# Second layer of a convolution and state-space network: token 6's input by compact sums, three products in column tiles, and a new written order

## The chip, the cores and the metric

The kernel runs on one core of a Trainium2 chip. The metric is the device time of one execution in microseconds (us), and the median of several runs stands for it. The engines are TensorE (PE), VectorE (DVE), ScalarE (ACT), GpSimd (POOL) and SyncE (SP), which here only issues transfers (DMAs). Each engine works through its own queue in order, and semaphores make it wait for the others. Matrix products land in PSUM, eight banks of 128 x 512 float32.

## The reference: what is computed

Two layers run on x of shape 8 x 128 x 128 x 128. The change touches only the second, which is this (cut):

```python
y = conv3x3(x, conv_w) + conv_b
seq = y.reshape(B * H * W, 8, 16)            # 8 tokens of 16 values
# in_proj, causal conv1d over tokens, silu -> xc [n, 8, 32]; z from the other half
dt, Bm, Cm = split(xc @ x_proj_w.T)          # 1, 16, 16 per token
dt = softplus(dt * dt_proj_w + dt_proj_b)
dA = exp(dt[..., None] * A)                  # [n, 8, 32, 16]
dBx = dt[..., None] * Bm[:, :, None, :] * xc[..., None]
h = dA[t] * h + dBx[t];  ys[t] = (h * Cm[t][:, None, :]).sum(-1)   # t = 0..7
out = ((ys + D * xc) * silu(z)) @ out_proj_w.T
out = x + silu(groupnorm(out))               # 4 groups, over the whole image
```

A sequence is one line of an image along its width: 128 values are 8 tokens of 16. For each of the 131072 sequences there is a state of 32 channels x 16, stepped through eight tokens from zero.

## The kernel before

The first layer ends at about 1950 us. The second works in 256 blocks, each of 4 image rows in all 128 channels (512 sequences). A block's state for one token is 32 x 16 = 512 rows of 512 sequences. It is cut into two chunks of 128 partitions x 2 x 512 (a chunk is called s, s = 2 t + half, so s runs from 0 to 15). The functions are steps, and the tuple ORDER gives the order in which one turn of the loop calls them: an entry is a step, the block it works on relative to the turn's block i, and its arguments. All five engines follow this order in their own queues (the schedule is manual), so a step's place is decided by hand, and nothing reorders it.

For a block, in the order of the data:

- conv (L137, in the helper _conv_taps): 9 taps, each a full-array product of 128 x 128 weights with 512 columns, into the only bank of "pm". biased and turn copy and transpose it.
- project_x, project_z, project_dt (L749, L761, L771) and project_bc (L789) give xc, z, dt and the rows of B and C. silu (ACT), softplus (L776), inputs u = dt * xc (L781, POOL), states (L796) take them out of PSUM.
- lay_states (L804) spreads each token's 16 rows of B ("bb") or C ("cc") over 128 partitions by transfers of 256 KB. store_inputs and lay_inputs (L814, L821) do so with u for the chunks that POOL injects.
- spread_a and spread_u (both L830): two products with 32 rows of the array each put dt * A, or u, of one chunk into one of three PSUM slots (2 banks each). Even chunks use the array's rows 0 to 63, odd ones rows 64 to 127.
- exps (L841, ACT) makes dA in place. inject makes h = u * B on DVE from PSUM (L853), or on POOL from a laid out copy (L851) for the chunks in BY_POOL = (4, 5, 10). decay multiplies dA by the earlier token's h in place (L861), add sums it into h (L866). weigh (L872, POOL) multiplies h by C.
- collect (L936): for each token, column-tiled products (32 columns of the array each, four side by side) sum over the 16 states into "yps".
- Tokens 0 and 7 are short cuts. Token 0's whole term and token 7's input term need no state: (sum over n of C B) * u. lay_ends and lay_own (L882, L891) gather the rows of B, C and u compactly, end_products (L896, POOL) multiplies B and C, ends_sum (L905, PE) sums over n, own_terms (L911, DVE) multiplies by u, own_add (L918, PE) adds into yps. Token 7's decayed part is dA7 * (C7 h6): weigh first, then decay (L859).
- skip (L929) starts yps with D * xc, gated (L943, DVE) multiplies by silu(z), project_out (L951) and result give the output. After an image's last block norm_of forms the group norm; last_load to last_store finish an earlier image beside the work. The last image is finished at the end.

PSUM holds the three slots (6 banks), pm (1) and yps (1). h tiles have 9 buffers, hc tiles 8, used in turn.

Of the kernel before, what the change touches and what calls it, by code (L numbers as in the profile page):

```python
# [16 lines left out]
P = 128  # L17
C = 128
# [21 lines left out]
def _fields(widths):  # L40
# [13 lines left out]
    ("half", NH * L), ("group", P), ("ends", 4 * NH * DI), ("place", 2 * NH * P),  # L54
# [13 lines left out]
def _constants():  # L68
# [4 lines left out]
    def put(c, fields, name, v):  # L73
# [34 lines left out]
    quarter, end = i % 4, i // (P // 2)  # L108
    put(c1, C1, "ends", np.stack([
        ((quarter == q) & (end == e))[:, None] & np.ones(DI, bool)[None, :] for q in range(4) for e in range(NH)], 1))  # L110
    put(c1, C1, "place", np.stack([
        (i // DI == h)[:, None] & (k[:, None] == i[None, :] // LP) & (i % LP == (0, LP - 1)[h % NH])[None, :]
        for h in range(2 * NH)], 1))
    put(c1, C1, "half", np.stack(
        [(i % LP)[:, None] + hf * LP == np.arange(L)[None, :] for hf in range(NH)], 1))
# [482 lines left out]
def layer1(ctx, tc, x1, w1, c1, out):  # L598
# [33 lines left out]
    ends = cf("ends").rearrange("p (q e d) -> p q e d", e=NH, d=DI)  # L632
# [56 lines left out]
    hcp = ctx.enter_context(tc.tile_pool(name="l1_hc", bufs=8))  # L689
# [6 lines left out]
    st8 = [{} for _ in blocks]  # L696
    xins, stats, gns, tails = {}, {}, {}, []
    LAST = (3, 6)
    BY_POOL = (4, 5, 10)
# [22 lines left out]
    def conv(i, k):  # L722
        d = st8[i]
        if k == 0:
            d["pm"] = misc()
        xin, lo = d["xin"]
        _conv_taps(nc, [d["pm"]], convw, [xin], lo, blocks[i][1], 1, k, k + 1)
# [17 lines left out]
    def project_x(i, slot):  # L745
        d = st8[i]
        d["ps"] = pair(slot)
        for hf in range(NH):
            nc.tensor.matmul(d["ps"][:, hf], m_xh[:, hf, :], d["yT"], start=True, stop=True)  # L749
# [18 lines left out]
    def project_dt(i, hf):  # L768
        d = st8[i]
        d["pm"] = misc()  # L770
        nc.tensor.matmul(flat(d["pm"]), m_dtf, d["xc"][:, hf, :], start=True, stop=True)  # L771
# [26 lines left out]
    def lay_states(i, hf, k):  # L798

        d, name = st8[i], ("bb", "cc")[k]  # L800
        v = wk2.tile([P, LP, N], F32, name=name)
        for t in range(hf * LP, (hf + 1) * LP):
            if t != (L - 1, 0)[k]:
                nc.sync.dma_start(  # L804
                    v[:, t % LP, :],
                    d["bc"[k]][t * DS:(t + 1) * DS, :].unsqueeze(1).broadcast_to([DS, 8, N]))
        d[name, hf] = v
# [35 lines left out]
    def state_row(i, name, t):  # L843
        return st8[i][name, t // LP][:, t % LP:t % LP + 1, :].broadcast_to([P, GP, N])
# [10 lines left out]
    def decay(i, s):  # L855
        d = st8[i]
        da = d["da", s]
        if s >= GP * (L - 1):
            nc.vector.tensor_mul(d["hc", s], da, d["hc", s])  # L859
        else:  # L860
# [12 lines left out]

    def lay_ends(i):
# [3 lines left out]
        d["bcs"] = wk1.tile([P, 2, C], F32, name="bcs")  # L878
        for k in range(2):
            src = d["bc"[k]].rearrange("p (q c) -> p q c", c=C)  # L880
            for e, t in enumerate((0, L - 1)):
                nc.sync.dma_start(d["bcs"][e * P // 2:(e + 1) * P // 2, k, :], src[t * DS:(t + 1) * DS])  # L882

    def lay_own(i):
        d = st8[i]
        d["us"] = wk1.tile([P, N // 2], F32, name="us")
        for e, l in enumerate((0, LP - 1)):
            u = d["u", e].rearrange("(d l) n -> l d n", l=LP)
            for h in range(2):
                a = (h * NH + e) * DI  # L890
                nc.sync.dma_start(d["us"][a:a + DI, :], u[l][:, h * (N // 2):(h + 1) * (N // 2)])  # L891

    def end_products(i):
        d = st8[i]
        d["cb"] = wk1.tile([P, C], F32, name="cb")
        nc.gpsimd.tensor_mul(d["cb"], d["bcs"][:, 0, :], d["bcs"][:, 1, :])  # L896

    def ends_sum(i):

        d = st8[i]  # L900
        d["pm"] = misc()
        for q in range(4):
            for e in range(NH):
                a = (q // 2 * NH + e) * DI
                nc.tensor.matmul(  # L905
                    d["pm"][a:a + DI, q % 2, :], ends[:, q, e, :], d["cb"], start=True, stop=True)
# [287 lines left out]
```

## Time and profile before

| | us |
|---|---|
| median of 3 runs | 13790.77 (13786.41 to 13790.79) |
| the profiled execution's own time | 13787.05 |
| its span, first to last instruction | 13785.2 |
| mean granted PE clock | 0.991 of full |
| first state operation of the second layer (inject) | 1968.6 |
| last block's output | 13707.1 |
| DVE decay, add (L861, L866), mean of one | 1.224, 1.220 |
| DVE inject from PSUM (L853), mean of one | 1.219 |
| POOL weigh (L872), mean of one | 2.365 |
| ACT exp (L841), mean of one; table load | 1.008; 1.283 |

A line of the profile names the engine, the line of the kernel, the operation and the tiles as out<-in, then how many and how long. Lengths of neighbouring operations on one engine overlap a little (an operation's start may lie before the end of the one ahead), so that what one costs in a full queue is the distance from its start to the next start. PE's lengths overlap much more, and products on different parts of the array run at once. "32*128" is a product that uses 32 of the array's rows and all its columns, "128*32" one with 32 of its columns.

### The profile page before, as it was taken

To read this page: it belongs to the slowest core of one execution; us is meant where nothing else is said; L and a number is where in the kernel's file an instruction comes from. 1 tells how busy PE (TensorE), PEld (TensorE's weight loads), DVE (VectorE), ACT (ScalarE), POOL (GpSimd) and SP (SyncE) were. 2 spreads that over 40 slices of the span, in tenths; PEclk is the share of its full clock that TensorE was granted. 3 is DMA by queue.
4 is the path that set the end of the run, shared out by engine and by line. 5 is a ranking of instruction groups with operands and counts; after the bars stand their busy time and mean duration, and the time that the engine had idled before them with its cause. 6 is when DMAs were issued, how large, how long until landed. Compare 5 with 4: busy or idle time off the path is not lost. (4 is left out here: it accounts for less than half of the span.)

```text
span 13785.2 us, 222858 instructions
## 1 busy us (share of the span) xinstructions
PE 13399.1 (97%) x80938; PEld 5420.6 (39%) x80938; DVE 12207.0 (89%) x11963; ACT 8884.5 (64%) x10881; POOL 12418.5 (90%) x6788
## 2 busy tenths in 40 slices
PE   9999999999999999999999999999999999999997
PEld 5676663333333333333333333333333333333332
DVE  3343359999999999999999999999999999999997
ACT  3454366666666666666666666666666666666665
POOL 6766669999999999999999999999999999999997
PEclk9999999999999999999999999999999999999998
DMA  4544456666667666666766666666666676667666
GB/s 134 159 133 126 142 133 139 139 137 137 147 155 158 153 152 155 156 156 149 158 154 157 154 153 155 156 156 151 156 156 155 150 158 154 158 148 158 154 156 179
DMA packets 1224332, 2078.57 MB, mean 151 GB/s; under 512 B 149568, under 2 KB 378944, under 8 KB 1215040
## 3 DMA queue, kind: packets, MB, share of 16 engines
q1 hardware_dynamic: 1222656, 2061.57, 64.5%
q8 instruction: 640, 10.49, 0.3%
q14 instruction: 460, 3.77, 0.1%
q10 hardware_dynamic: 576, 2.74, 0.1%
HBM read 822.20 MB, written 234.88 MB: 77 GB/s over the span
## 5 line engine op out<-in xcount | busy, mean ns | idle before, releaser
L872 POOL TENSOR_TENSOR hc<-h,cc 128x1024 f32<-128x1024 f32 x3584 | 8377.6, 2365 | 523.5 <-PE pm L905 409.5
L841 ACT ACTIVATE s<-s 128x1024 f32<-128x1024 f32 x3584 | 3589.5, 1008 | 2879.1 <-PE s L830 2727.0
L830 PE MATMUL s<-dt,m_a 32*128 32x512 f32 x14336 | 3967.9, 638 | 25.8 <-DVE h L866 13.9
L866 DVE TENSOR_TENSOR h<-s,h 128x1024 f32<-128x1024 f32 x3072 | 3726.2, 1220 | 71.4 <-DVE s L861 1.4
L861 DVE TENSOR_TENSOR s<-s,h 128x1024 f32<-128x1024 f32 x3072 | 3738.0, 1224 | 2.8 <-ACT s L841 2.7
L853 DVE TENSOR_TENSOR h<-s,bb 128x1024 f32<-128x1024 f32 x2816 | 3431.9, 1219 | 224.6 <-PE s L830 111.8
L830 PE MATMUL s<-u,l_ct 32*128 32x512 f32 x11264 | 3164.1, 638 | 143.7 <-DVE h L853 134.6
L137 PE MATMUL pm<-xin,l_wt 128*128 128x508 f32 (+1 forms) x4608 | 2341.6, 617 | 6.1 <-DVE wk L652 5.4
L936 PE MATMUL yps<-hc,l_ct 128*32 128x512 f32 x14336 | 1852.6, 602 | 2.7 <-ACT away L969 2.7
L851 POOL TENSOR_TENSOR h<-ud,bb 128x1024 f32<-128x1024 f32 x768 | 1808.5, 2370 | 11.5 <-DMA ud<-uw 11.5
L830 PEld LDWEIGHTS s<-dt,m_a 32*128 32x128 f32 x14336 | 1105.0, 183 | 1432.6 <-DVE h L866 532.5
L830 PEld LDWEIGHTS s<-u,l_ct 32*128 32x128 f32 x11264 | 867.8, 184 | 1371.9 <-DVE h L853 555.3
L137 PEld LDWEIGHTS pm<-xin,l_wt 128*128 128x128 f32 x4608 | 771.5, 189 | 1478.2 <-issue 1260.5
L841 ACT ACT_TABLE_LOAD x774 | 993.0, 1283 | 29.1 <-DVE h L853 11.0
L936 PEld LDWEIGHTS yps<-hc,l_ct 128*32 128x32 f32 x14336 | 362.3, 109 | 1140.6 <-issue 1061.6
L781 POOL TENSOR_TENSOR u<-dt,xc 128x512 f32<-128x512 f32 x512 | 649.9, 1269 | 77.5 <-ACT dt L776 46.8
L776 ACT ACT_TABLE_LOAD x511 | 655.6, 1283 | 50.5 <-PE pm L771 9.8
L859 DVE TENSOR_TENSOR hc<-s,hc 128x1024 f32<-128x1024 f32 x512 | 622.1, 1215 | 2.8 <-ACT s L841 2.8
L771 PE MATMUL pm<-xc,m_dt 128*128 128x512 f32 x1024 | 583.8, 652 | 1.4 <-ACT yT L743 0.7
L951 PEld LDWEIGHTS pm<-m_o,ym 128*128 128x128 f32 x4096 | 476.5, 191 | 194.5 <-ACT dt L776 192.7
L918 PE MATMUL yps<-own,l_ct 128*32 128x256 f32 x8192 | 542.2, 382 | 0.1
L789 PE MATMUL pm<-xc,m_bc 128*32 128x512 f32 x4096 | 539.3, 598 | 2.3 <-ACT all_b L796 1.4
(195 smaller groups left out, 13183.6 us busy)
## 6 DMA issues: line engine op xcount, KB each, us to landing
bb<-all_b SPq DMA_DIRECT2D x1792, 256.0 KB, 5.6
cc<-all_c SPq DMA_DIRECT2D x1792, 256.0 KB, 5.8
ud<-uw SPq DMA_DIRECT2D x1536, 256.0 KB, 4.6
xin<-x SPq DMA_DIRECT2D x152, 768.0 KB, 5.1
xin<-x SPq DMA_DIRECT2D x112, 640.0 KB, 6.9
gn<-xr SPq DMA_DIRECT2D x256, 256.0 KB, 5.4
v<-gn SPq DMA_DIRECT2D x224, 256.0 KB, 3.0
res<-x SPq DMA_DIRECT2D x224, 256.0 KB, 3.1
```

Source lines behind the costliest of these rows:

```text
L137: nc.tensor.matmul(out[:, a:b, wa:wb], wt[:, t, :], src[:, r + dy + a - base:r + dy + b - base, wa + dx:wb + dx], start=(n == 0), stop=(n ...
L776: nc.scalar.activation(d["dt", hf], flat(d["pm"]), AF.Softplus, bias=wf("dt_b"))
L781: nc.gpsimd.tensor_mul(d["u", hf], d["dt", hf], d["xc"][:, hf, :])
L830: nc.tensor.matmul(d[name, s][:, q], m[a:a + DI, t % LP, :], d[src, t // LP][a:a + DI, :], start=True, stop=True)
L841: nc.scalar.activation(da, da, AF.Exp)
L851: nc.gpsimd.tensor_mul(h, d["ud", t][:, k:k + GP, :], state_row(i, "bb", t))
L853: nc.vector.tensor_mul(h, d["ups", s], state_row(i, "bb", t))
L859: nc.vector.tensor_mul(d["hc", s], da, d["hc", s])
L861: nc.vector.tensor_mul(da, da, d["h", s - GP])
L866: nc.vector.tensor_add(h, d["da", s], h)
L872: nc.gpsimd.tensor_mul(hc, d["h", s if t < L - 1 else s - GP], state_row(i, "cc", t))
L936: nc.tensor.matmul(d["yps"][g * DI:(g + 1) * DI], gather[:, t % LP, :], d["hc", GP * t + g // GP][:, g % GP], start=False, stop=t in LAST, ...
```

## The change

- Token 6's input no longer goes through the state. What y6 takes from it is (sum over n of C6 B6) * u6, what y7 takes is (sum over n of dA7 C7 B6) * u6. So chunks 12 and 13 have no spread_u, inject and add; their decay writes dA6 * h5 straight into h. A new DVE step, cross, multiplies dA7 of chunks 14 and 15 by a broadcast of C7 B6 ("cbx", laid out by the new lay_cross), and ends_sum sums it by four gather products more.
- The compact terms have four items now: token 0 of the next block, token 6, token 7, and the cross term. bcs is 256 wide, us and own are 512 wide. lay_first and lay_own_first bring the next block's token 0.
- POOL no longer injects chunk 10; DVE does, from PSUM.
- bb and cc tiles hold only the tokens that are needed, in one buffer each. hc tiles have 9 buffers, used by cross too.
- The convolution, project_x and project_dt are made of four column tiles of 32 instead of one full-array product (every call has wide = 0).
- ORDER is a new one.

The diff, cut to its core:

```diff
-    hcp = ctx.enter_context(tc.tile_pool(name="l1_hc", bufs=8))
+    hcp = ctx.enter_context(tc.tile_pool(name="l1_hc", bufs=9))
+    ROWS = {("bb", 0): (0, 4), ("bb", 1): (4, 6), ("cc", 0): (1, 4), ("cc", 1): (4, 8)}
-    BY_POOL = (4, 5, 10)
+    BY_POOL = (4, 5)
+    def tiles_of(wide):
+        return [slice(0, P)] if wide else [slice(q * DI, (q + 1) * DI) for q in range(P // DI)]
...
-        _conv_taps(nc, [d["pm"]], convw, [xin], lo, blocks[i][1], 1, k, k + 1)
+        for c in tiles_of(wide):
+            nc.tensor.matmul(
+                d["pm"][c, a:b, wa:wb], convw[:, t, c], xin[:, r + dy + a - lo:r + dy + b - lo, wa + dx:wb + dx],
+                start=(k == 0), stop=(k == len(taps9) - 1), skip_group_check=True)
...
-            nc.tensor.matmul(d["ps"][:, hf], m_xh[:, hf, :], d["yT"], start=True, stop=True)
+            for c in tiles_of(wide):
+                nc.tensor.matmul(d["ps"][c, hf], m_xh[:, hf, c], d["yT"], start=True, stop=True)
...
-        v = wk2.tile([P, LP, N], F32, name=name)
+        v = wk1.tile([P, t1 - t0, N], F32, name=f"{name}{hf}")
...
+        elif s >= GP * (L - 2):
+            h = d["h", s] = hp.tile([P, GP, N], F32, name="h")
+            nc.vector.tensor_mul(h, da, d["h", s - GP])
...
+    def cross(i, s):
+        d = st8[i]
+        cr = d["cr", s] = hcp.tile([P, GP, N], F32, name="hc")
+        nc.vector.tensor_mul(cr, d["da", s], d["cbx"].broadcast_to([P, GP, N]))
...
+            nc.sync.dma_start(d["bcs"][DI:3 * DI, k, :], src[(L - 2) * DS:L * DS])
+            nc.sync.dma_start(d["bcs"][3 * DI:4 * DI, k, :], src[t * DS:(t + 1) * DS])
+    def lay_first(i):
+        d, nx = st8[i], st8[min(i + 1, nb - 1)]
+        for k in range(2):
+            src = nx["bc"[k]].rearrange("p (q c) -> p q c", c=N // 2)
+            nc.sync.dma_start(d["bcs"][0:DI, k, :], src[0:DS])
...
+        us = d["us"].rearrange("(d j) n -> j d n", j=LP)
+        u = d["u", 1].rearrange("(d l) n -> l d n", l=LP)
+        for j, l in ((1, LP - 2), (2, LP - 1), (3, LP - 2)):
+            nc.sync.dma_start(us[j], u[l])
...
+    def lay_cross(i):
+        d = st8[i]
+        d["cbx"] = wk1.tile([P, 1, N], F32, name="cbx")
+        cb = d["cb"].rearrange("(i n q) c -> i q n c", n=DS, q=2)[3]
+        for q in range(2):
+            nc.sync.dma_start(
+                d["cbx"][:, 0, q * (N // 2):(q + 1) * (N // 2)],
+                cb[q].unsqueeze(1).broadcast_to([DS, 8, N // 2]))
...
+        for g in range(NG if i >= 0 else 0):
+            nc.tensor.matmul(
+                flat(pm)[g * DI:(g + 1) * DI], gather[:, LP - 1, :], d["cr", GP * (L - 1) + g // GP][:, g % GP],
+                start=True, stop=False, skip_group_check=True)
+        for q in range(2):
+            for g in range(NG):
+                nc.tensor.matmul(
+                    flat(pm)[g * DI:(g + 1) * DI, q * (N // 2):(q + 1) * (N // 2)], ends[:, q, :], d["cb"],
+                    start=i < 0, stop=True, skip_group_check=True)
...
-        d["own"] = wk2.tile([P, N // 2], F32, name="own")
-        nc.vector.tensor_mul(d["own"], flat(d["pm"])[:, 0:N // 2], d["us"])
+        d["own"] = wk2.tile([P, N], F32, name="own")
+        nc.vector.tensor_mul(d["own"], flat(d["pm"]), d["us"])
...
+        own = st8[i - 1 + hf]["own"]
+        for g in range(NG):
+            a = slice(g * DI, (g + 1) * DI)
+            nc.tensor.matmul(d["yps"][a], place[:, hf, a], own, start=False, stop=False, skip_group_check=True)
```

The new ORDER:

```python
ORDER = (
    (load, 4), (store_inputs, 0, 2), (last_store, -2), (exps, -1, 10), (lay_first, -1), (end_products, -1),
    (exps, -1, 13), (lay_own, -1), (add, -1, 11), (conv, 2, 0, 0), (project_z, 1, 0), (silu_z, 1),
    (decay, -1, 10), (decay, -1, 13), (conv, 2, 1, 0), (add, -1, 10), (weigh, -1, 8), (spread_u, 0, 2, 2),
    (spread_a, -1, 15, 1), (gated, -1, 0), (inject, 0, 2), (spread_a, -1, 12, 0), (conv, 2, 2, 0),
    (exps, -1, 15), (lay_cross, -1), (weigh, -1, 15), (lay_inputs, 0, 2), (weigh, -1, 13), (weigh, -1, 10),
    (project_x, 1, 2, 0), (exps, -1, 12), (lay_states, 0, 1, 0), (silu_x, 1), (decay, -1, 15),
    (decay, -1, 12), (cross, -1, 15), (conv, 2, 3, 0), (spread_u, 0, 1, 0), (spread_a, 0, 2, 1),
    (spread_u, 0, 7, 2), (exps, 0, 2), (inject, 0, 1), (conv, 2, 4, 0), (skip, -1, 1), (spread_u, 0, 3, 0),
    (inputs, 0, 1), (inject, 0, 7), (spread_a, -1, 14, 2), (exps, -1, 14), (conv, 2, 5, 0),
    (collect, -1, 4), (decay, 0, 2), (inject, 0, 3), (conv, 2, 6, 0), (weigh, -1, 14), (add, 0, 2),
    (spread_a, 0, 3, 0), (lay_states, 0, 0, 1), (spread_u, 0, 8, 1), (cross, -1, 14), (conv, 2, 7, 0),
    (last_act, -1), (lay_ends, 0), (weigh, -1, 11), (decay, -1, 14), (collect, -1, 5), (inject, 0, 8),
    (weigh, -1, 12), (exps, 0, 3), (decay, 0, 3), (conv, 2, 8, 0), (keep, -2), (spread_u, 0, 9, 1),
    (spread_a, 0, 4, 2), (lay_own_first, -1), (add, 0, 3), (biased, 2), (inject, 0, 4), (norm, -3),
    (turn, 2), (exps, 0, 4), (inject, 0, 9), (decay, 0, 4), (last_load, 0), (turned, 2),
    (spread_a, 0, 6, 0), (exps, 0, 6), (spread_of, -2), (ends_sum, -1), (weigh, 0, 2), (spread_a, 0, 5, 1),
    (add, 0, 4), (own_terms, -1), (exps, 0, 5), (inject, 0, 5), (decay, 0, 6), (spread_u, 0, 6, 2),
    (project_dt, 1, 0, 0), (inject, 0, 6), (decay, 0, 5), (collect, -1, 7), (spread_a, 0, 7, 2),
    (collect, -1, 6), (softplus, 1, 0), (exps, 0, 7), (project_bc, 1, 0), (weigh, 0, 3), (own_add, -1, 1),
    (lay_states, 0, 1, 1), (inputs, 1, 0), (states, 1, 0), (add, 0, 6), (last_sum, -1), (weigh, 0, 4),
    (add, 0, 5), (decay, 0, 7), (gated, -1, 1), (spread_u, 0, 11, 1), (spread_a, 0, 8, 0), (skip, 0, 0),
    (add, 0, 7), (project_bc, 1, 1), (weigh, 0, 5), (exps, 0, 8), (inject, 0, 11), (collect, 0, 1),
    (decay, 0, 8), (spread_u, 0, 10, 2), (lay_states, 1, 0, 0), (states, 1, 1), (weigh, 0, 7),
    (spread_a, 0, 9, 1), (inject, 0, 10), (add, 0, 8), (project_dt, 1, 1, 0), (own_add, 0, 0),
    (exps, 0, 9), (decay, 0, 9), (collect, 0, 2), (spread_a, 0, 11, 0), (softplus, 1, 1), (add, 0, 9),
    (spread_u, 1, 0, 2), (project_out, -1, 0), (inject, 1, 0), (weigh, 0, 6), (project_out, -1, 1),
    (exps, 0, 11), (result, -1), (spread_a, 0, 10, 1), (decay, 0, 11), (spread_a, 0, 13, 2), (weigh, 0, 9),
    (collect, 0, 3),
)
```

## Prediction

> **What bounds the kernel now.** I read the page's busy line, then stretches of the second layer, then the period of one block, then each engine's instructions in order of time inside one period.
>
> ```profile
> PE 13399.1 (97%) x80938; PEld 5420.6 (39%) x80938; DVE 12207.0 (89%) x11963; ACT 8884.5 (64%) x10881; POOL 12418.5 (90%) x6788
> ```
>
> ```profile
> 8000.00:9000.00 1000.00, 988.28 (x5958) 354.93 (x5957) 979.73 (x883) 685.57 (x796) 964.02 (x465) 1.00 0.70 156
> ```
>
> ```profile
> L911 DVE TENSOR_TENSOR own<-pm,us x3: 415/415/417, 8005.4 to 8096.0; 128x256 f32<-128x256 f32 x3
> ```
>
> In the second layer (about 1943 to 13707 us) PE is busy 98.8%, DVE 98.0%, POOL 96.4%, ACT 68.6%. A block takes (8096.0 - 8005.4) / 2 = 45.3 us, and there are 256. So three queues are nearly full, and a gain has to shorten all three.
>
> PE's timeline (start, length, operation):
>
> ```profile
> 8006.57 1.06 PE L789 MATMUL pm<-xc,m_bc 128*32 128x512 f32 x8
> 8007.46 1.04 PE L936 MATMUL yps<-hc,l_ct 128*32 128x512 f32 x8
> 8008.32 1.05 PE L918 MATMUL yps<-own,l_ct 128*32 128x256 f32 x16
> 8009.18 1.04 PE L789 MATMUL pm<-xc,m_bc 128*32 128x512 f32 x8
> 8010.15 1.13 PE L830 MATMUL s<-u,l_ct 32*128 32x512 f32 x4
> ...
> 8020.91 1.12 PE L137 MATMUL pm<-xin,l_wt 128*128 128x512 f32 x2
> 8021.96 0.70 PE L830 MATMUL s<-u,l_ct 32*128 32x512 f32 x2
> 8021.98 0.70 PE L830 MATMUL s<-dt,m_a 32*128 32x512 f32 x2
> ...
> 8023.03 1.12 PE L137 MATMUL pm<-xin,l_wt 128*128 128x508 f32 x2
> 8024.18 1.13 PE L830 MATMUL s<-dt,m_a 32*128 32x512 f32 x4
> ```
>
> Read starts, not lengths. Column-tiled jobs (128*32) follow each other in 0.86 us; leaving that shape costs about 0.13 more (8009.18 to 8010.15). A full-array tap between spreads takes 1.05 to 1.15. Two spreads of opposite parity (different 32-row strips) run together in 1.07, an unpaired one takes about 1.06.
>
> DVE:
>
> ```profile
> 8025.08 1.22 DVE L861 TENSOR_TENSOR s<-s,h 128x1024 f32<-128x1024 f32 x1
> 8026.34 1.23 DVE L866 TENSOR_TENSOR h<-s,h 128x1024 f32<-128x1024 f32 x1
> 8027.48 1.22 DVE L861 TENSOR_TENSOR s<-s,h 128x1024 f32<-128x1024 f32 x1
> ```
>
> An add right behind the decay that it reads starts 1.26 us after it; otherwise the step is 1.13.
>
> **The change, part by part**, per block.
>
> DVE. Two adds (L866) go, the injects of chunks 12 and 13 go, the inject of chunk 10 comes over from POOL, and two cross products arrive, the same 128x1024 from PSUM as an inject: 37 large operations become 36. own is 512 wide instead of 256; its step goes from 0.33 to the 0.60 of the equally wide gated product (L943). Sum: 36 x 1.131 + 3 x 0.60 = 42.5. The new order puts four adds right behind their decay (chunks 3, 4, 9, 11): 4 x 0.126 = 0.5. That makes 43.0; the old sum without waits is 37 x 1.131 + 0.33 + 1.20 = 43.4, and its period of 45.3 holds 1.9 of dependent steps and waits.
>
> POOL. 17 large products become 16 at 2.32 (in POOL's timeline eight in a row took 18.59 us): 37.1; inputs 2 x 1.23, last sum 1.24; end_products is 256 wide, between its 0.41 for 128 and 1.23 for 512, so 0.69. Sum 41.5 instead of 43.6.
>
> PE. Convolution, x and dt (9 + 2 + 2 units of 512 columns) took 9.4 + 1.8 + 2.1 = 13.4 us, from each start to the next operation's in PE's timeline. In four column tiles they have the shape of L936. "TensorEngine Tiling (Array Packing)", section Performance Considerations, recommends column tiling where the left operand's free dimension is at most 64; here it is 128, so by that rule four times the instructions buy nothing. The row agrees that the work isn't shorter (0.86 for four tiles; two full-array taps together, 8032.58 to 8034.48, took 0.95 each). What they buy is company: they now stand next to collects, and 26 column units (9 convolution, 2 x, 2 dt, 7 collect, 2 bc, 2 own, and the end sum, which grows from 0.57 to 2 units) lie in 11 runs: 26 x 0.86 + 11 x 0.13 = 23.8. By the rule alone PE would keep 13.4 and grow by 1.2. Spreads go from 25 (17.6 us, much of it waiting for PSUM slots) to 24; the order has 10 pairs, 2 singles behind a pair and 2 alone: 10.7 + 1.7 + 2.1 = 14.5. With z 1.06, turn 0.59 and output 1.93 PE needs 41.9.
>
> ACT. silu of z, silu of x and the last silu are now parted by exps, so there are 10 table loads a block instead of 6.
>
> ```profile
> 8013.27 1.28 ACT L776 ACT_TABLE_LOAD   x1
> 8014.57 0.69 ACT L776 ACTIVATE dt<-pm,l_wt 128x512 f32<-128x512 f32 x1
> 8015.27 1.28 ACT L841 ACT_TABLE_LOAD   x1
> 8016.57 1.01 ACT L841 ACTIVATE s<-s 128x1024 f32<-128x1024 f32 x1
> ```
>
> A load adds 1.29 and no more: 31.1 + 4 x 1.29 = 36.3, under 44. The page "ScalarE: Activation LUTs", What ACT_TABLE_LOAD costs, adds about 1.38 of drain to every switch; ten drains would make ACT 50 and the bound. The rows above leave no room for one, so I take 36.3.
>
> SP and transfers. Per block 34.5 issues before and after: one bb row, two ud rows, one uw store and a few small ones go; two cbx broadcasts and other small ones come. Bytes fall by about 0.3 of 7 MB, so the transfers' load of 0.70 doesn't grow. Only cbx is short of time. Its neighbours:
>
> ```profile
> cc<-all_c SPq DMA_DIRECT2D x155, 256.0 KB, 5.8
> us<-u SPq DMA_DIRECT2D x88, 32.0 KB, 2.3
> bcs<-all_b SPq DMA_DIRECT2D x44, 32.0 KB, 3.9
> ```
>
> cbx is two of 128 KB in cc's broadcast shape. SP issues took 0.6 typically, up to 2.2 behind a wait. After end_products both land within 0.6 + 2.0 = 2.6 (too good) to 2.2 + 0.6 + 5.8 = 8.6 us; I take 5.8, between the last two rows. On DVE cross 15 waits for it, and behind it stand injects 1 and 7 and decay 2, and PE's spread a2, which needs its slot.
>
> **The walk.** Full queues meet in waits, so I walked the new order once around with these steps, each read from start to start in the timelines: PE to exp 1.2 (8021.98 to 8023.19), exp to DVE 1.09 (8039.29 to 8040.38), DVE to the PSUM slot's next spread 1.27 (8036.79 to 8038.06). Zero is decay 10: decay 13 at 1.13, add 10 at 2.26, gated at 3.39, inject 2 at 3.99; decay 15 could start at 5.12. But spread a15 needs add 10's slot: PE at 3.53, and the exp's table load waits for the same slot, so exp at 4.82, decay 15 at 5.91: 0.8 lost. Then decay 12, cross 15 (8.16); inject 1 could start at 9.29, but PE first does a12, conv, x, x, conv to 8.4, plus 1.18: 0.3 lost. From there each operand was ready, by 0.1 at decays 3 and 7. DVE's cycle is 43.0 + 1.1 = 44.1. PE in the same walk loses 0.4 to 0.6 where a pair's second slot comes late (a14, u6, a9), 41.9 + about 2 = 44. POOL waits 2.3 for an hc buffer until collect 7 (weigh 3 reuses weigh 15's) and ends at 43.8. So end_products ends 7.5 before cross 15, and cbx has 1.7 to spare.
>
> Sum: (45.3 - 44.1) x 256 = 310 us of the profiled execution's 13787.05 (span 13785.2), which stands 3.7 below the median 13790.77. Forecast 13790.8 - 310 = 13480. The seven image boundaries (about 11.5 us extra each), the last image's tail and the fill and drain stay; I allow 20 either way, since the same steps are there in another rotation.
>
> **Rivals.**
> - Main case, 0.71: period 43.7 to 44.6, 13380 to 13610.
> - The waits of the walk vanish (latencies overlap more than single rows show) and DVE's 43.0 to 43.6 is the period: 13200 to 13350. For: PE needs only 41.9. Against: the loop add 10, a15, exp 15, decay 15 is serial. 0.09.
> - The old order's kind of loss stays: it lost 1.9 on DVE over its sum, the new one may lose 2.2 to 2.7 over 42.5 as ties slip; period 44.7 to 45.2, 13640 to 13760, or level with before. 0.13, of which 0.03 within 0.2%.
> - Slower: cbx comes late. Its slack is 1.7 us; cross 15 then holds DVE's whole queue. By the upper bound (8.6) DVE loses 1.1, period 45.2, just even. It decides from a landing about 8.7 us after end_products; at 10 us the loss is 2.5, the period 46.6, the time 14120. Against: half of cc's bytes at a load of 0.70. 0.07, together with anything like it.
>
> That the change doesn't do what it says: the order on each engine shows 36 large DVE and 16 large POOL products, so the removal is real.
>
> **Numbers.** A measurement of this kernel tells about 0.2% (28 us) from no change. Faster 0.90, same 0.03, slower 0.07. Range 13300 to 13690: the main case, the floor's upper third (0.03), half of the remaining losses (0.06), which is 0.80.
>
> **What would show it.** Own's interval should be 44.1. DVE's decay of chunk 15 should wait about 0.8 for its exp, the inject of chunk 1 about 0.3 for PE. Convolution between collects should step in 0.86. ACT should show 10 loads of 1.28 a block without drains. cross should show no wait for a transfer; if it does, the last rival has it. If PE, not DVE, has no idle time left, the pairs came apart more than walked. I am wrong if column-tiled taps take clearly over 0.9, or if losses in the walk's ties add up.

## The result and the profile after

| us | before | after |
|---|---|---|
| median (lowest to highest) | 13789.55 (13786.41 to 13790.79) | 13595.74 (13593.01 to 13599.65) |
| ratio, with 95% interval | | 0.986 (0.9843 to 0.9877) |
| span of the profiled execution | 13785.2 | 13594.9 |
| mean granted PE clock | 0.991 | 0.99 |
| period of a block, mean without image boundaries | 45.33 | 44.56 |

The kernel is faster by 194 us, 1.4%; the forecast was 310. The clock is the same, so it is the work that changed. A period is here the distance between two neighbouring own products on DVE. Leaving out the seven blocks in which an image begins, it fell by 0.77 us, and 249 times 0.77 is 192 of the span's 190. The boundary blocks take what they took (56 to 58 us), and fill and drain give nothing net: all of it lies in the usual block.

The page after, busy time of each engine:

```profile
PE 13227.2 (97%) x97850; PEld 4812.6 (35%) x97850; DVE 11943.4 (88%) x11710; ACT 10091.1 (74%) x11827; POOL 11940.1 (88%) x6533
```

The same stretch of the second layer (length, then PE, PEld, DVE, ACT, POOL busy, the granted clock, the transfers' load, GB/s):

```profile
8000.00:9000.00 1000.00, 991.59 (x7541) 308.50 (x7532) 972.44 (x877) 811.02 (x898) 937.84 (x450) 1.00 0.64 151
```

And the own products in a stretch without an image boundary:

```profile
L964 DVE TENSOR_TENSOR own<-pm,us x25: 678/680/682, 7906.3 to 8975.8; 128x512 f32<-128x512 f32 x25
```

24 periods in 1069.5 us are 44.56 each. PE and DVE are still as good as full, POOL has come down to 93.8%, the transfers' load from 0.70 to 0.64, and ACT is up to 81%.

DVE's timeline (start, length, operation, idle time before it):

```profile
8018.41 0.68 DVE L994 TENSOR_TENSOR ym<-yps,zs 128x512 f32<-128x512 f32 x1
8019.01 1.21 DVE L864 TENSOR_TENSOR h<-s,bb 128x1024 f32<-128x1024 f32 x1
8020.98 1.23 DVE L870 TENSOR_TENSOR hc<-s,hc 128x1024 f32<-128x1024 f32 x1 [0.76 <-ACT s L851]
8022.12 1.21 DVE L873 TENSOR_TENSOR h<-s,h 128x1024 f32<-128x1024 f32 x1
8023.25 1.21 DVE L892 TENSOR_TENSOR hc<-s,cbx 128x1024 f32<-128x1024 f32 x1
8024.56 2.41 DVE L864 TENSOR_TENSOR h<-s,bb 128x1024 f32<-128x1024 f32 x2
...
8028.02 1.21 DVE L864 TENSOR_TENSOR h<-s,bb 128x1024 f32<-128x1024 f32 x1
...
8033.74 1.23 DVE L875 TENSOR_TENSOR s<-s,h 128x1024 f32<-128x1024 f32 x1
...
8037.28 1.22 DVE L875 TENSOR_TENSOR s<-s,h 128x1024 f32<-128x1024 f32 x1
8038.60 1.23 DVE L880 TENSOR_TENSOR h<-s,h 128x1024 f32<-128x1024 f32 x1
8039.74 0.68 DVE L964 TENSOR_TENSOR own<-pm,us 128x512 f32<-128x512 f32 x1
...
8042.61 1.22 DVE L875 TENSOR_TENSOR s<-s,h 128x1024 f32<-128x1024 f32 x1
8043.74 2.34 DVE L880 TENSOR_TENSOR h<-s,h 128x1024 f32<-128x1024 f32 x2
8046.18 1.23 DVE L875 TENSOR_TENSOR s<-s,h 128x1024 f32<-128x1024 f32 x1
```

Three things stand here. The decay of chunk 15 (L870) starts 1.97 behind inject 2 instead of 1.13: the forecast wait for its exp, 0.84. Inject 1 (8024.56) starts 1.31 behind cross (L892), so it waits 0.18, and cross 15 itself follows decay 12 in 1.13, so it doesn't wait for its transfer. In the lower part the view marks no idle time, yet two steps are long: decay 4 (8037.28) to add 4 takes 1.32, and the two adds at 8043.74 (chunks 6 and 5) take 2.44 until decay 7, which is 1.13 and 1.31. Decay 7 reads the h5 that add 5 has just written. The idle time in these steps is about 0.1 (decay 4 ends at 8038.50, add 4 starts at 8038.60), too short for the view to mark it; only the distance between starts shows the step. The rows at 8028.02 (inject 3) and 8033.74 (decay 3) come up again with the cross term.

PE's timeline, a tap and the spread for inject 1, then the convolution and collect with a pair of spreads behind them:

```profile
8022.23 1.03 PE L734 MATMUL pm<-xin,l_wt 128*32 128x508 f32 x8
8023.39 1.13 PE L840 MATMUL s<-u,l_ct 32*128 32x512 f32 x4
...
8028.08 1.06 PE L734 MATMUL pm<-xin,l_wt 128*32 128x508 f32 x8
8028.96 1.04 PE L987 MATMUL yps<-hc,l_ct 128*32 128x512 f32 x8
8029.82 1.03 PE L734 MATMUL pm<-xin,l_wt 128*32 128x508 f32 x8
8030.78 0.70 PE L840 MATMUL s<-dt,m_a 32*128 32x512 f32 x2
8030.80 0.70 PE L840 MATMUL s<-u,l_ct 32*128 32x512 f32 x2
```

A tap in column tiles steps in 0.88 and a collect in 0.86; leaving the shape adds about 0.1 (8029.82 to 8030.78). The tap at 8022.23 is followed by its spread only after 1.16: PE was free about 0.12 earlier, and the spread starts when decay 12 on DVE (8022.12 for 1.21) has ended and so freed its PSUM slot. Inject 1 follows when the spread is done. So inject 1 doesn't wait for PE's queue but for a handover, decay 12, slot, spread, inject, of 2.44 us in all.

ACT's timeline:

```profile
8015.72 1.28 ACT L776 ACT_TABLE_LOAD   x1
8017.02 1.02 ACT L776 ACTIVATE zs<-s 128x1024 f32<-128x1024 f32 x1
8018.57 1.28 ACT L851 ACT_TABLE_LOAD   x1 [0.53 <-DVE h L880]
8019.86 1.93 ACT L851 ACTIVATE s<-s 128x1024 f32<-128x1024 f32 x2
8021.81 1.28 ACT L764 ACT_TABLE_LOAD   x1
8023.10 1.11 ACT L764 ACTIVATE xc<-s,l_wt 128x1024 f32<-128x1024 f32 x1
```

Each load is followed by its operation 1.29 to 1.30 after its start, and the one at 8021.81 begins when the exps ahead of it are over (8021.79). There is no drain, as in the rows of before. The load at 8018.57 didn't run ahead: it waited for DVE's add 10 (which ends at 8018.49), whose slot the exp behind it needs.

Among the transfers, cbx (issues, KB, median us from issue to landing):

```profile
cbx<-cb SPq DMA_DIRECT2D x46, 128.0 KB, 2.4
```

It lands 2.4 us after its issue. The forecast was for the whole way from the end of end_products to the second landing, 2.6 (too good) to 8.6: in the trace that is 3.05 (median of all blocks), and cross 15 comes 5.1 after the landing. The waits of POOL (us in total, times, longest) in 8000 to 9000:

```profile
POOL u L792 <- ACT dt L787: 25.1, 23, 1.5
...
POOL hc L886 <- PE s L840: 19.0, 22, 0.9
...
POOL cb L935 <- DMA bcs<-all_c: 14.0, 12, 2.6
```

The last one comes 12 times in some 22 blocks: in every second block end_products waits for the compact rows of C. The blocks with this wait take as long as those without it, 44.49 both, so here it costs nothing.

### The profile page after: what moved, and what is told of

Same layout as the page of the kernel before. It is cut to its first block, busy times and chain, and to the rows that moved or that the text cites. A ratio compares the mean times of both kernels' runs of the same rounds, so it can differ in the third digit from the quotient of the medians.

```text
span 13594.9 us, 255193 instructions
## 1 busy us (share of the span) xinstructions
PE 13227.2 (97%) x97850; PEld 4812.6 (35%) x97850; DVE 11943.4 (88%) x11710; ACT 10091.1 (74%) x11827; POOL 11940.1 (88%) x6533
## 5 line engine op out<-in xcount | busy, mean ns | idle before, releaser
L840 PE MATMUL s<-dt,m_a 32*128 32x512 f32 x14336 | 3525.2, 638 | 17.0 <-DVE h L880 14.5
L875 DVE TENSOR_TENSOR s<-s,h 128x1024 f32<-128x1024 f32 x2560 | 3134.3, 1224 | 46.0 <-ACT s L851 22.4
L864 DVE TENSOR_TENSOR h<-s,bb 128x1024 f32<-128x1024 f32 x2560 | 3100.6, 1215 | 55.2 <-DMA bb<-all_b 20.2
L840 PE MATMUL s<-u,l_ct 32*128 32x512 f32 x10240 | 2892.2, 641 | 50.2 <-DVE h L873 18.4
L734 PE MATMUL pm<-xin,l_wt 128*32 128x508 f32 (+3 forms) x18432 | 2409.2, 595 | 6.2 <-DVE wk L650 5.5
L862 POOL TENSOR_TENSOR h<-ud,bb 128x1024 f32<-128x1024 f32 x512 | 1220.8, 2384 | 2.4 <-DMA ud<-uw 2.4
L734 PEld LDWEIGHTS pm<-xin,l_wt 128*32 128x32 f32 x18432 | 469.3, 109 | 1588.4 <-issue 1586.7
L870 DVE TENSOR_TENSOR hc<-s,hc 128x1024 f32<-128x1024 f32 x512 | 623.6, 1218 | 199.4 <-ACT s L851 191.0
L980 ACT ACTIVATE yps<-xc,l_wt 128x512 f32<-128x512 f32 x511 | 352.1, 689 | 403.3 <-DVE ym L994 403.3
L892 DVE TENSOR_TENSOR hc<-s,cbx 128x1024 f32<-128x1024 f32 x512 | 620.4, 1212 | 0.0
L782 PE MATMUL pm<-xc,m_dt 128*32 128x512 f32 x4096 | 545.6, 605 | 1.4 <-ACT yT L752 0.7
```

Source lines behind the costliest of these rows:

```text
L734: nc.tensor.matmul(d["pm"][c, a:b, wa:wb], convw[:, t, c], xin[:, r + dy + a - lo:r + dy + b - lo, wa + dx:wb + dx], start=(k == 0), stop= ...
L840: nc.tensor.matmul(d[name, s][:, q], m[a:a + DI, t % LP, :], d[src, t // LP][a:a + DI, :], start=True, stop=True)
L862: nc.gpsimd.tensor_mul(h, d["ud", t][:, k:k + GP, :], state_row(i, "bb", t))
L864: nc.vector.tensor_mul(h, d["ups", s], state_row(i, "bb", t))
L875: nc.vector.tensor_mul(da, da, d["h", s - GP])
```

## Experiments

The theory: the period is set by DVE's queue together with PE's, tied by the PSUM slots; the column tiles and the new order gained, and what is missing of the forecast is small steps and waits on DVE. Rivals: PE alone is the bound; ACT's four new table loads took the rest; POOL or the transfers of the compact terms hold it up. All ratios are to the kernel before on the same chip; the usual period is the median one (in the last two kernels from ACT's copy of own).

| kernel | median us | ratio (95%) | usual period |
|---|---|---|---|
| before | 13789.55 | 1 | 45.32 |
| after | 13595.74 | 0.986 (0.9843 to 0.9877) | 44.49 |
| columns_old_order | 13740.80 | 0.9965 (0.9952 to 0.9978) | 45.11 |
| full_new_order | 13721.66 | 0.9952 (0.9937 to 0.9967) | 45.03 |
| compact_old_order | 14812.32 | 1.0741 (1.0725 to 1.0757) | 49.29 |
| both_old_order | 14841.14 | 1.0764 (1.0746 to 1.0782) | 49.05 |
| both_old_order_2 | 14412.75 | 1.0454 (1.0438 to 1.047) | 47.61 |
| pe_more | 13741.08 | 0.9966 (0.9953 to 0.9978) | 45.10 |
| dve_more | 13771.95 | 0.9988 (0.9981 to 0.9995) | 45.21 |
| pool_more | 13592.82 | 0.9857 (0.9844 to 0.9871) | 44.50 |
| no_tables | 13533.77 | 0.9815 (0.98 to 0.983) | 44.28 |
| no_cross | 13565.08 | 0.9837 (0.9823 to 0.985) | 44.44 |
| own_moved | 13531.91 | 0.9813 (0.98 to 0.9827) | 44.10 |
| own_moved_2 | 13496.64 | 0.9787 (0.9773 to 0.98) | 44.09 |

**Column tiles alone, in the old order.** The kernel before, with the convolution, x and dt in four tiles:

```diff
-        _conv_taps(nc, [d["pm"]], convw, [xin], lo, blocks[i][1], 1, k, k + 1)
+        for q in range(4):
+            c = slice(q * DI, (q + 1) * DI)
+            nc.tensor.matmul(
+                d["pm"][c, a:b, wa:wb], convw[:, t, c], xin[:, r + dy + a - lo:r + dy + b - lo, wa + dx:wb + dx],
+                start=(k == 0), stop=(k == 8), skip_group_check=True)
...
+                nc.tensor.matmul(d["ps"][c, hf], m_xh[:, hf, c], d["yT"], start=True, stop=True)
...
+            nc.tensor.matmul(flat(d["pm"])[c], m_dtf[:, c], d["xc"][:, hf, :], start=True, stop=True)
```

> The kernel before, with its order and its sums, and only the convolution, x and dt products made of four column tiles. Theory (column tiles save only where a tap stands beside another column job, and PE alone can't shorten the block because DVE is full too): in the old order most taps stand between spreads, where a column unit costs 0.99 instead of 1.06; block 45.1 to 45.4 us, total 13740 to 13800, no change that can be told. Rival (the column tiles are where the gain comes from, as PE was the bound): at least 0.4 us a block less, 13690 or below. Second rival (four times the instructions cost on PE): above 13820.

It gains 49 us, 0.2 a block: at the fast end of the expected range, but a change that can be told. Its stretch:

```profile
8000.00:9000.00 1000.00, 983.76 (x7704) 330.47 (x7706) 983.77 (x887) 688.17 (x799) 970.88 (x466) 1.00 0.70 157
```

DVE and POOL, which do the old work, are fuller than before (98.4% and 97.1%), and PE is less full (98.4%). So with 37 large operations left on DVE little more can come from PE; its gain alone is worth 0.35%.

**The new order without column tiles.**

```diff
     def tiles_of(wide):
-        return [slice(0, P)] if wide else [slice(q * DI, (q + 1) * DI) for q in range(P // DI)]
+        return [slice(0, P)]
```

> The changed kernel with the convolution, x and dt as full-array products again, order as changed. Theory (column tiles buy company: taps between collects then change the array's shape twice): about 7 more changes of shape of 0.13 to 0.2 and 6 dearer exits, 1.0 to 1.8 us of PE a block, of which waits inside PE's queue take up some; 0.5 to 1.6 us a block, 13720 to 14010. Rival (tiles make no difference, only the removed operations count): 13580 to 13630.

It loses 126 us of the 194, at the near end of what was expected. PE is 99.86% busy in 8000 to 9000 (after: 99.16%), so here it has no slack. PE's timeline of it, dt between others:

```profile
8030.83 1.13 PE L782 MATMUL pm<-xc,m_dt 128*128 128x512 f32 x2
8031.88 1.07 PE L971 MATMUL yps<-own,l_ct 128*32 128x512 f32 x8
8032.77 1.04 PE L987 MATMUL yps<-hc,l_ct 128*32 128x512 f32 x8
```

and of the kernel after, the same place:

```profile
8006.89 1.07 PE L782 MATMUL pm<-xc,m_dt 128*32 128x512 f32 x8
8007.77 1.04 PE L971 MATMUL yps<-own,l_ct 128*32 128x512 f32 x8
8008.63 1.04 PE L987 MATMUL yps<-hc,l_ct 128*32 128x512 f32 x8
```

1.05 against 0.88 for the same product. A full-array tap ahead of a collect took 1.05 as well (in column tiles 0.88), the collect between two taps 0.995 instead of 0.86, and the tap behind it 1.05 instead of 0.96. Even a tap with spreads on both sides stepped in 0.98 to 0.99 instead of 1.05, so company isn't the whole of it. The rule of the Trainium skill, "TensorEngine Tiling (Array Packing)", section Performance Considerations, recommends column tiles where the left operand has at most 64 columns; here it has 128, so the rule gave no reason to expect a gain, and these rows show one. The two parts help each other: tiles alone 49, order and sums alone 68, together 194. That fits two queues that both have to shrink: with the tiles alone DVE is left full, with the order alone PE.

**Compact sums in the old order.** I fitted the compact steps into the old ORDER: spread, inject and add of chunks 12 and 13 taken out, chunk 10's spread and inject put where chunk 13's had stood, cross behind the decays of 15 and 14, the transfers of the compact rows ahead of their first reader. Once with full-array products, once with column tiles.

```diff
-        (states, 1, 1), (spread_u, 0, 13, 0), (decay, 0, 8), (inject, 0, 13), (skip, 0, 0), (add, 0, 8),
+        (states, 1, 1), (spread_u, 0, 10, 0), (decay, 0, 8), (inject, 0, 10), (skip, 0, 0), (add, 0, 8),
...
-        (inject, 0, 10), (inject, 1, 1), (lay_ends, 1), (exps, 0, 10), (weigh, 0, 9), (add, 0, 11),
+        (inject, 1, 1), (lay_first, 0), (end_products, 0), (lay_cross, 0), (lay_ends, 1), (exps, 0, 10), (weigh, 0, 9), (add, 0, 11),
...
-        (silu_z, 2), (store_inputs, 1, 2), (add, 0, 12), (spread_a, 0, 15, 2), (spread_u, 1, 3, 0),
+        (silu_z, 2), (store_inputs, 1, 2), (spread_a, 0, 15, 2), (spread_u, 1, 3, 0),
...
+        (decay, 0, 15), (cross, 0, 15),
...
+        (decay, 0, 14), (cross, 0, 14),
```

> The new sums (token 6 by compact sums, cross, four items in own, chunk 10 on DVE, one buffer for bb and cc) with full-array products and the old order, adapted only where the new steps need a place. Theory (each full queue has to shrink; DVE loses 0.9 of work and POOL 2.1, but PE keeps its mode changes and gets 0.6 more from the end sum): 44.6 to 45.4 us a block, 13620 to 13810. Rival (the operations taken off DVE and POOL are the whole gain): 44.5 a block, 13600, as the changed kernel. Second rival (the old order's waits don't fit the new steps): above 45.6, 13870 or more.

> As the last one, with the column tiles too: the changed kernel's work in the old order. Theory: the order matters as much as the work, because what is left are waits; 44.6 to 45.4 us a block, 13620 to 13810, slower than the changed kernel by 20 to 200. Rival (the new order adds nothing beyond the removed work): within 30 us of the changed kernel's 13596. Second rival (the new order's ten table loads a block cost): faster than 13570.

Both are over 7% slower than before. The first was expected so by its second rival only, the second by none. The column tiles won nothing in this order: with them it is 29 us slower. The waits of POOL in both_old_order:

```profile
POOL hc L885 <- PE yps L989: 151.1, 19, 9.3
```

About 7.5 us a block, weigh 12 stands before an hc buffer that collect 4 frees: cross takes hc buffers too, and with 9 of them the old place of collect 4 is late. I put that down to my fitting, not to the compact sums. So I moved the two steps that free buffers:

```diff
         (cross, 0, 15),
+        (skip, 0, 1),
...
         (inject, 1, 7),
+        (collect, 0, 4),
         (conv, 3, 6, 0),
...
-        (skip, 0, 1),
...
-        (collect, 0, 4),
```

> The changed kernel's work in the old order once more, with the wait that spoiled the first try taken away: POOL's product for chunk 12 waited 7 to 9 us a block for an hc buffer that collect 4 frees, so collect 4 and the start of its sum now stand earlier. Theory (what the new order saves is waits, beyond the work): 44.9 to 46.0 us a block, 13700 to 13980. Rival (the order adds nothing of its own): within 40 us of 13596.

14412.75 us: better by 428, and a miss for both theories. POOL's wait was down from 151 to 79 us in the same stretch, 3.7 a block, but in DVE's timeline:

```profile
8008.34 1.22 DVE L872 TENSOR_TENSOR h<-s,h 128x1024 f32<-128x1024 f32 x1
8009.71 1.22 DVE L872 TENSOR_TENSOR h<-s,h 128x1024 f32<-128x1024 f32 x1 [0.16 <-ACT s L851]
8013.51 1.23 DVE L864 TENSOR_TENSOR h<-s,bb 128x1024 f32<-128x1024 f32 x1 [2.57 <-PE s L840]
```

The step to the next block's first inject is 3.80. In the kernel before, the adds of chunks 13 and 12 stood behind these two decays, and only 0.28 was waited ahead of that inject (add 12, then the inject):

```profile
8028.74 1.22 DVE L866 TENSOR_TENSOR h<-s,h 128x1024 f32<-128x1024 f32 x1
8030.25 1.23 DVE L853 TENSOR_TENSOR h<-s,bb 128x1024 f32<-128x1024 f32 x1 [0.28 <-PE s L830]
```

The work that was removed had covered the wait for the spread. This shows that removed operations can turn into waits nearly one for one; it doesn't show what the best order in the old style would give, which stays open.

**One more PE product.** The first tap of the convolution is made twice (one unit of 0.88 more a block).

```diff
-        for c in tiles_of(wide):
+        for c in tiles_of(wide) * (2 if k == 0 else 1):
```

> The changed kernel with one column unit more on PE a block: the first tap is computed twice (the second time from the start, so the output stays). Theory (PE and DVE are bound to each other by the PSUM slots, and PE has no free place): the unit's 0.88 and the pair u2, a15 that it pushes apart reach DVE's inject of chunk 1: 0.7 to 1.05 us a block, 13770 to 13860. Rival (DVE alone is the bound, PE's 0.8 of waits takes the unit in): 0 to 0.3 us, 13590 to 13670.

It costs 145 us, 0.57 a block: between the theory's range and the rival's, so both missed. DVE's timeline:

```profile
8007.79 0.68 DVE L994 TENSOR_TENSOR ym<-yps,zs 128x512 f32<-128x512 f32 x1
8009.19 1.23 DVE L864 TENSOR_TENSOR h<-s,bb 128x1024 f32<-128x1024 f32 x1 [0.72 <-issue]
...
8012.81 1.21 DVE L892 TENSOR_TENSOR hc<-s,cbx 128x1024 f32<-128x1024 f32 x1
8014.61 2.35 DVE L864 TENSOR_TENSOR h<-s,bb 128x1024 f32<-128x1024 f32 x2 [0.60 <-PE s L840]
```

Inject 2 now waits 0.8 (0 in after) and inject 1 0.67 (0.18 in after), while the wait of decay 15 shrinks to about 0.2. So a PE product comes through to the end for two thirds, and the rest is taken by waits that were there. PE is 99.6% busy now and no longer idle before the spread of inject 1: in this kernel PE is the bound, while in after it was idle for about 0.3 a block (0.17 before collect 1, 0.12 before the spread of inject 1).

**One more DVE product.** The gated product of half 1 is made twice (0.60 more).

```diff
+        if hf == 1:
+            nc.vector.tensor_mul(d["ym", hf], d["yps"], d["zs"][:, hf, :])
```

> The changed kernel with the gated product of the second half computed twice, 0.60 us more on DVE a block. Theory (DVE's queue is the cycle; its one long wait, before decay 15, has a fixed length behind add 10 and takes nothing in): the full 0.6, 13730 to 13770. Rival (PE is the bound and DVE's 1 us of waits takes it in): 0 to 0.2 us, 13590 to 13650.

It costs 176 us, 0.69 a block: all of it and a little more, as the second product follows the first, which writes the same tile, in 0.72 instead of 0.60. Every other step of DVE is as in after, the wait of decay 15 (0.83) and that of inject 1 (0.18) too. By itself this run doesn't clear PE, since the product also holds yps longer: the wait of PE's collect 1 behind it grew from 0.17 to 0.96 a block. The run without own on DVE, below, decides.

**One more POOL product.** inputs of half 1 is made twice (1.23 more).

```diff
+        if hf == 1:
+            nc.gpsimd.tensor_mul(d["u", hf], d["dt", hf], d["xc"][:, hf, :])
```

> The changed kernel with one of POOL's input products computed twice, 1.24 us more on POOL a block. Theory (POOL isn't a bound after the change: 2.8 us of waits a block, and its next inject lands 1.6 us before its add): 0 to 0.15 us a block, 13580 to 13640. Rival (three queues are full, POOL too): 0.6 to 1.24 us, 13750 to 13910.

13592.82, no different from after. POOL's 2.8 us of waits a block took it; it is no bound.

**No table loads.** Silu of the second layer is replaced by the identity and softplus by exp, so that all share one table; the result is then another function.

```diff
-        nc.scalar.activation(d["zs"], d["pz"], AF.Silu)
+        nc.scalar.activation(d["zs"], d["pz"], AF.Identity)
...
-        nc.scalar.activation(d["dt", hf], flat(d["pm"]), AF.Softplus, bias=wf("dt_b"))
+        nc.scalar.activation(d["dt", hf], flat(d["pm"]), AF.Exp, bias=wf("dt_b"))
```

> The changed kernel's second layer with Identity in place of silu and Exp in place of softplus: another function, the same operations and sizes on ACT, and none of the ten table loads a block. Theory (the loads only stretch ties: exp 7 behind softplus, exp 15 and exp 3 behind silu): 0.2 to 0.4 us a block less, 13490 to 13550. Rival (the loads hide entirely): 13580 to 13610. Second rival (the six became ten loads, and their 12.9 us are what ate the forecast's missing 0.4 and more): below 13450.

All ten loads, 12.8 us of ACT a block (busy time fell from 811 to 525 in 1000), are worth 62 us, 0.24 a block. Decay 15's wait fell from 0.83 to 0.69, and decay 3's of 0.06 went. So the four loads that the change adds took at most that, and ACT isn't the bound. The long step to decay 7 stayed 1.31: ACT's tables have nothing to do with it.

**No cross term.** Both cross steps, lay_cross and the gather products are left out; token 6's share in y7 is then missing.

```diff
-        for g in range(NG if i >= 0 else 0):
+        for g in range(0):
...
-        (exps, -1, 15), (lay_cross, -1), (weigh, -1, 15), (lay_inputs, 0, 2), (weigh, -1, 13), (weigh, -1, 10),
+        (exps, -1, 15), (weigh, -1, 15), (lay_inputs, 0, 2), (weigh, -1, 13), (weigh, -1, 10),
...
-        (decay, -1, 12), (cross, -1, 15), (conv, 2, 3, 0), (spread_u, 0, 1, 0), (spread_a, 0, 2, 1),
+        (decay, -1, 12), (conv, 2, 3, 0), (spread_u, 0, 1, 0), (spread_a, 0, 2, 1),
```

> The changed kernel without the cross term: no lay_cross, no cross products on DVE (2 x 1.13), no gather of them on PE (0.9); token 7 loses the part of token 6's input. Theory (PE and DVE are bound to each other; behind cross 15 DVE waits for PE's spread u1 anyway, behind cross 14 for u8 and exp 3): only 0.05 to 0.4 us a block, 13490 to 13590. Rival (each operation on DVE's queue costs its length): 2.3 us, 13000 to 13100. Second rival (PE is the bound): 0.9 us, 13340 to 13390.

2.26 us of DVE and 0.9 of PE less a block, and the time falls by 31 us, 0.1 a block, as the theory expected. DVE's timeline:

```profile
8002.97 1.22 DVE L870 TENSOR_TENSOR hc<-s,hc 128x1024 f32<-128x1024 f32 x1 [0.75 <-ACT s L851]
8004.12 1.21 DVE L873 TENSOR_TENSOR h<-s,h 128x1024 f32<-128x1024 f32 x1
8006.56 2.35 DVE L864 TENSOR_TENSOR h<-s,bb 128x1024 f32<-128x1024 f32 x2 [1.23 <-PE s L840]
...
8009.96 1.21 DVE L864 TENSOR_TENSOR h<-s,bb 128x1024 f32<-128x1024 f32 x1
...
8013.96 1.23 DVE L864 TENSOR_TENSOR h<-s,bb 128x1024 f32<-128x1024 f32 x1 [0.52 <-PE s L840]
8015.68 1.23 DVE L875 TENSOR_TENSOR s<-s,h 128x1024 f32<-128x1024 f32 x1 [0.50 <-ACT s L851]
```

Waits of 1.23, 0.52 and 0.50 stand behind the places of the two products. Start to start these steps lose 2.5, where after loses 0.3 in the same places: nearly all of the 2.26 came back as waits. Two of the three are for a spread, yet PE isn't full here (98.4% busy) and was itself idle for 0.12 before the spread of inject 1. What holds DVE are two handovers that took the same time in both kernels. From decay 12 to inject 1 it is 2.44 (8004.12 to 8006.56; in after 8022.12 to 8024.56): slot, spread, inject. From inject 3 to decay 3 it is 5.72 (8009.96 to 8015.68; in after 8028.02 to 8033.74): ACT waits for inject 3, then come a table load, the last silu, another load and exp 3. The wait of inject 8 for PE lies inside the second and isn't its last one. The cross products ran in the shade of these two.

**own off DVE.** The own product goes: ACT copies pm out, POOL multiplies.

```diff
-        nc.vector.tensor_mul(d["own"], flat(d["pm"]), d["us"])
+        nc.scalar.copy(d["own"], flat(d["pm"]))
...
+    def own_times(i):
+        d = st8[i]
+        nc.gpsimd.tensor_mul(d["own"], d["own"], d["us"])
...
-        (collect, -1, 6), (softplus, 1, 0), (exps, 0, 7), (project_bc, 1, 0), (weigh, 0, 3), (own_add, -1, 1),
+        (collect, -1, 6), (softplus, 1, 0), (exps, 0, 7), (project_bc, 1, 0), (weigh, 0, 3), (own_times, -1), (own_add, -1, 1),
```

> The changed kernel with own's product taken off DVE: ACT copies the end sums out of PSUM (0.59, in a gap before exp 5) and POOL multiplies by u in place (1.23, behind the product for chunk 3, where POOL waits 0.8 to 1.5 for softplus). Theory (DVE and PE bind each other, and both have work behind this place that waits for a slot): DVE's 0.60 less brings 0.3 to 0.6 us a block, 13440 to 13520. Rival (PE is full, nothing): 13580 to 13610. Second rival (POOL, 94% busy, is as full as the others): 13620 to 13800.

It gains 64 us: 0.39 in the usual block, 0.25 in the mean; 13531.91 lies between the ranges of the theory and of its rival. In the usual block DVE's steps are those of after but for this place: own's 0.60 is gone, and decay 6 now stands right behind add 4, whose result it reads, so that this step became 1.33 instead of 1.13 and 0.2 of the 0.6 came back. The 0.4 that is left came through whole, while PE's work stayed the same: PE wasn't the bound in after, DVE with its handovers was. In the mean something more is lost: the first image's 32 blocks still take 44.69, and of the 212 later blocks without an image boundary 50 are over 0.1 longer than the usual one, up to 46.8, 29 us in all (in after 26 with 10 us). POOL, fuller now, still waits in every second block (its waits):

```profile
POOL cb L935 <- DMA bcs<-all_c: 17.3, 12, 2.0
```

SP's queue shows why every second one: the load of the next input rows stands ahead of the compact rows, and comes once in two blocks. So the last kernel sends the compact rows first:

```diff
-        (load, 4), (store_inputs, 0, 2), (last_store, -2), (exps, -1, 10), (lay_first, -1), (end_products, -1),
+        (lay_first, -1), (load, 4), (store_inputs, 0, 2), (last_store, -2), (exps, -1, 10), (end_products, -1),
```

> own_moved, and the two transfers of lay_first issued ahead of the next image rows' load on SP. In own_moved every second block, the one with that load, POOL's end_products waits 1.5 us for them, and the mean block is 0.25 us longer than the usual one. Theory (the wait is SP's order: the transfers stand behind a load, a store and a result): it goes, 0.1 to 0.25 us a block, 13460 to 13510. Rival (POOL is simply full at 97%, and the wait turns up elsewhere): 13520 to 13545.

13496.64 us, 0.9787 (0.9773 to 0.98) of before and 99 below after: the fastest kernel here. The wait of end_products is gone. The usual period is the same (44.09, before it 44.10); what changed is that 18 blocks are longer, with 7 us in all, instead of 50 with 29, and that the image boundaries became about 1 us shorter each. Its stretch:

```profile
8000.00:9000.00 1000.00, 997.20 (x7618) 312.93 (x7612) 970.65 (x863) 832.60 (x929) 975.79 (x478) 1.00 0.65 152
```

PE is at 99.7% now, and POOL at 97.6% is close.

## Why the prediction was right in its sign and too large in its size

DVE's period, term by term (measured as steps from start to start in the usual block):

| term, us a block | forecast | measured |
|---|---|---|
| 36 large and 3 small operations | 42.5 | 42.5 |
| dependent steps beyond 1.13 | 0.5 | 0.77 |
| decay 15 for its exp | 0.8 | 0.83 |
| inject 1 for its spread | 0.3 | 0.18 |
| inject 7, decay 3, and steps some 10 ns over 1.131 | 0 | 0.19 |
| blocks longer than the usual one (mean less usual) | 0 | 0.07 |
| mean period | 44.1 | 44.56 |

- **The period of before** held: 45.33 by 45.3.
- **The mechanism** held in the main: DVE's queue with its handovers sets the period, PE follows close behind, the column tiles count, and the walk's two waits are where it put them, with the sizes it gave them within 0.12. What DVE's removed operation brings by itself wasn't measured: order and sums were only run together. DVE's sum fell by 0.87 (43.38 to 42.51), and the usual period by 0.83, so what the order loses over the sum hardly changed (1.94 before, 1.98 after).
- **Inject 1's wait** is right in size partly by luck. The walk had PE late with its own products (8.4 behind decay 10). PE was ready at 8.2 and waited for the slot that decay 12 frees at 8.3.
- **The term that was mis-sized** is "four adds right behind their decay: 4 x 0.126 = 0.5". There are five dependent steps, and two are longer than the 1.26 that I had read from one row: decay 9 to add 9 and decay 11 to add 11 0.125 each, decay 3 to add 3 0.136, decay 4 to add 4 0.195, and add 5 to decay 7 0.185. The trace of before had such a longer step in plain view, decay 10 to add 10 at 8021.48 and 8022.81 (1.33). I had looked for adds behind their decays only, and not for a decay behind the add that makes its h. own_moved made another one (add 4 to decay 6, 1.33 in the place of 1.13), and no_tables left this one as it was, so it goes with the dependence. That taking these steps apart would bring their 0.77 back wasn't tried. How much of it would come stays open: own_moved's 0.4 came whole, but PE is 99.6% busy there.
- **"From there each operand was ready, by 0.1 at decays 3 and 7"** was too tight: 0.06 each was lost at decay 3 and inject 7. No_tables brought the one at decay 3 back, so it came from ACT, whose two loads stand ahead of exp 3.
- **What was left out**: lay_first behind the input's load on SP. I had counted SP's issues and the bytes, but not which compact transfer stands behind the large one. In after it costs nothing that can be seen; where POOL was fuller, own_moved_2 gained 35 us over own_moved by removing it. The 0.07 between mean and usual period lies elsewhere: the first image's blocks take 44.69, and 26 later blocks are 0.1 to 1.1 longer. Why is open.
- **A reading that was off**: the busy shares that the prediction gives for the whole second layer (98.8, 98.0, 96.4 and 68.6%) are those of 8000 to 9000. From 1943 to 13707 they are 98.1, 97.2, 94.7 and 67.5%. And its rows give 0.11, not 0.13, for leaving column tiles. Neither moves the forecast of DVE's period.
- The sum: the forecast of the period was 0.46 too short, and 0.46 x 256 is 118 of the 116 us between forecast and result.
- **PE**: a tap ahead of a collect stepped in 0.88 and the collect in 0.86, as forecast; the tap that leaves the run took 0.96. full_new_order shows this part's worth in the new order, 126 us. The rival that PE alone is the bound falls by own_moved; that PE doesn't matter falls by pe_more and full_new_order.
- **ACT**: 81.1% of 44.56 is 36.1, forecast 36.3. The drain of about 1.38 at each switch that the Trainium skill states ("ScalarE: Activation LUTs", section What ACT_TABLE_LOAD costs) isn't in this trace.
- **The rivals**: "the waits vanish" is out, since both waits are there. "cbx comes late" is out, 3.05 us for the whole way and no wait. "The old order's kind of loss stays" was partly right: the order lost 2.0 over its sum in the usual block and 2.05 in the mean, between the main case's 1.6 and that rival's 2.2.

## What to carry to other kernels

When you walk a written order, mark every operation that stands right behind the one whose result it reads, of whatever kind, and read the step for each kind from the trace, start to start: such steps appear in no list of waits. Where in-order engines hand buffers to each other, added and removed work don't count alike: here 0.60 more on DVE cost 0.69, 0.88 more on PE 0.57, and 2.26 less on DVE gave 0.1. So look for the handovers around an operation (which operation frees the buffer, which engines it passes through, which operation it comes back to), measure their length start to start, and judge the operation by whether it stands in the shade of one. And when an order or a shape is undone alone, expect a remainder: here tiles and order gave 49 and 68 us apart and 194 together.

## What was not expected of the hardware

- A dependent step on DVE isn't one number: 1.26 (add 9, add 11) and 1.31 to 1.33 (add 4, decay 7, decay 6 in own_moved) for the same 128x1024 operation that steps in 1.13 otherwise. The rows follow one pattern: ahead of each of the longer ones a semaphore instruction of 0.02 us stands in DVE's queue (at 8038.54 and 8046.12 in after, 8022.75 in before), and the operation also reads what another engine made (POOL's inject 4 or 10, ACT's exp 6 or 7); ahead of add 9 and add 11 there is none, and they read only what DVE wrote. The idle time is 0.10 against 0.03. That the second engine is the cause wasn't tried by a run of its own.
- Splitting a full 128 x 128 product into four column tiles makes it cheaper next to other column-tiled work: 0.88 instead of 1.05 ahead of a collect, and the collect 0.86 instead of 0.995.
- A load of an activation table took 1.29 us and nothing else, but one waited for the slot that the operation behind it needs (0.53 at 8018.57), so that it wasn't hidden in that wait.
- Two broadcasts of 128 KB landed in 2.4 us (2.3 to 3.7) at a load of 0.64, while the 256 KB of cc took 5.5 in the same stretch. That is half the size in less than half the time; why wasn't tested.
